# Two transposes move from TensorE to DMA: layer 1's mask and layer 3's result, with a retuned instruction order

## The chip, the cores and the metric

The kernel runs on one core of one Trainium2 chip. The metric is the device time of one execution in microseconds: the median of three runs, 3709.41 us before the change (3707.99 to 3712.8). A core has TensorE (PE in the profile; PEld is its weight load), VectorE (DVE), ScalarE (ACT), GpSimd (POOL), and SyncE (SP), which here issues all the transfers to 16 DMA engines.

## The reference, cut to what matters

The input is 64 graphs of 256 nodes with 256 features each, and a 256x256 adjacency for each graph. Four layers follow, each with a layer norm and ReLU ahead and a residual after. All of it is float32.

```python
for layer in (L0, L1, L2, L3):
    h = maximum(layernorm(x), 0)
    x = x + layer(h, adj)

# L0: attention with 8 heads, masked by adj, softmax over keys, output weights Wo
# L1: one head. e[i,j] = leaky_relu(f1[i] + f2[j]), masked by adj
#     softmax over axis 1 (over i, for each j), then h' = attention @ Wh, elu
# L2: three steps of message passing:  m = h W_l;  aggr = A^T m;  h = GRU(aggr, h)
# L3: four heads of 64 features:
f = (h @ W.T + b).reshape(B, N, H, c)
logits = leaky_relu(s_src[:, :, None, :] + s_dst[:, None, :, :])
probs  = softmax(where(adj == 1, logits, NEG_INF), axis=2)
out    = einsum('bijh,bjhc->bihc', probs, f).reshape(B, N, H * c)
```

Layer 1's softmax runs over i for each j. The kernel therefore holds j on the partitions, and needs the mask, which arrives with i on the partitions, turned. Layer 3's product comes out of TensorE with features on the partitions, and has to be turned before it is added to x, which has nodes on the partitions.

## The kernel before

The kernel takes two graphs at a time, a pair, 32 pairs in all. A tile `w4` is 128 partitions x 1024 float32: 4 tiles of 128 nodes (T = 4, two for each graph) by 256. Every piece of work is a task with the engine or engines that can do it, a modelled duration, and the buffers it reads and writes. When the kernel is built, a list scheduler with fixed constants puts the tasks in one static order for each engine, so that up to five pairs are in work at once and the long layer 2 fills gaps.

```python
# constants of the scheduler (times in us, and offsets in its priority)
SPARE, GRAIN = 5, 0.001          # w4 tiles kept back for the oldest pair
SLOW, MARGIN = 1.5, 0.4          # factor on a transfer's latency; extra ahead of SyncE
BACK = {"DVE": 0.3, "POOL": 0.6} # for work that two engines can do
PERIOD, REST = 698.4, 0
ON_PE = (-200, 1975, 7842, -3606)     # offset by layer, TensorE
ON_SP = (5643, 3540, 5173, -3294)
OTHERS = (2505, 934, 848, 4291)

SLOTS = {  # tag: (tiles, shape, type, reserve)
    "x": (5, [P, T * D], FP, 0),    "w4": (30, [P, T * D], FP, 9),
    "mask": (4, [P, T * N], BF, 1), "w2": (4, [P, N2], FP, 2),   # N2 = 512
    "ps": (8, [P, 512], FP, 2),     # PSUM banks
    ...
    "turn": (8, [P, T * N], FP, 0), # in DRAM
}
```

Most turns of attention matrices and of layer 2's state go through DRAM already: VectorE transposes 32x32 blocks, one transfer writes the tile out, and four transfers read it back with the blocks in their places. Only the last pair turns them on TensorE.

```python
def by_dma(l, p):
    return p < B // 2 - 1           # for all three steps of layer 2

def through_dram(e, eT):
    d = buf("turn")
    dma(d, e)                                              # 512 KB
    for b in range(4):                                     # 128 KB each
        dma(eT[32*b : 32*b+32].rearrange("p (a w) -> p a w", a=4),
            d[:, b*N : (b+1)*N].rearrange("(a j) w -> j a w", a=4))

def turn(e, eT):
    nc.vector.transpose(blocks(e), blocks(e)); through_dram(e, eT)
```

(The code above is shortened to its calls; `dma` stands for a task on SyncE.) Layer 1 builds a bfloat16 mask, computes the logits while a row of them goes through DRAM to all partitions, and turns the mask on TensorE into a PSUM bank:

```python
# layer 1
add((V, ..., m1 = (adj <= 0) * MASKED), reads=[at, hT], writes=[m1])     # bfloat16, [P, 4*256]
# ... Wh = h W; f1, f2; f1 as a row -> DRAM -> all partitions; e = prelu(f1 + f2)
psb = bank()
def turn_mask():
    for g in range(2):
        for cj in range(2):
            for ci in range(2):
                nc.tensor.transpose(                                     # L829
                    psm()[:, 2 * g + cj, ci * P : (ci + 1) * P],
                    tok(m1(), N)[:, 2 * g + ci, cj * P : (cj + 1) * P], identb)
add((PE, 8 * 0.058, turn_mask), reads=[m1, e], writes=[psb])
# logits: e = mask + e, with the row minimum of the negative, on VectorE, reading psm()
```

Layer 3 ends, for each graph g of the pair, with

```python
pso, oT = bank(), buf("w2")
add((PE, 1.86, product), reads=[*eT, (f, 2*g), (f, 2*g+1)], writes=[pso], claims=[oT])  # L1120
add(evict(N2, oT, pso), reads=[pso], writes=[oT])          # copy PSUM -> SBUF: ACT or VectorE
psq, o = bank(), buf("w2")
def back(psq=psq, oT=oT):
    for i in range(2):
        for k in range(2):
            nc.tensor.transpose(                                          # L1136
                psq()[:, i*D + k*P : i*D + (k+1)*P], oT()[:, k*N + i*P : k*N + (i+1)*P], ident)
add((PE, 4 * TURN, back), reads=[oT], writes=[psq], claims=[o, rz])
add((V, dve(N2), o = psq * rz), reads=[psq, rz], writes=[o])              # L1143, 1 / sum of exp
add(either(0.0, x_half += o), reads=[o], writes=[(xt, g)])                # L1148, VectorE or GpSimd
```

Of the kernel before, what the change touches and what calls it, by code (L numbers as in the profile page):

```python
# [9 lines left out]
FP = mybir.dt.float32  # L10
BF = mybir.dt.bfloat16
I32 = mybir.dt.int32
AF = mybir.ActivationFunctionType
ALU = mybir.AluOpType
AX = mybir.AxisListType

P = 128
# [21 lines left out]
class Plan:  # L39
# [11 lines left out]

    SPARE, GRAIN = 5, 0.001
    SLOW, MARGIN = 1.5, 0.4
    BACK = {"DVE": 0.3, "POOL": 0.6}


    PERIOD, REST = 698.4, 0
    ON_PE = (-200, 1975, 7842, -3606)  # L60
    ON_SP = (5643, 3540, 5173, -3294)
    OTHERS = (2505, 934, 848, 4291)

    def __init__(self, slots, spare):
        self.slots, self.spare = slots, spare
# [121 lines left out]
def tile_adj_preln_d4(  # L187
# [27 lines left out]
    nc = tc.nc  # L215
    B, N, D = x.shape
    NL = ggw.shape[0]
    H0, H3 = 8, a3.shape[0]
    D0, C3 = D // H0, D // H3
    assert N == 2 * P and D == 2 * P and B % 2 == 0 and H0 == 8 and H3 == 4  # L220
    T = 4
    N2 = 2 * N
# [3 lines left out]
    const = ctx.enter_context(tc.tile_pool(name="const", bufs=1))  # L226

    SLOTS = {
        "x": (5, [P, T * D], FP, 0),
        "w4": (30, [P, T * D], FP, 9),  # L230
        "f3": (2, [P, T, E3], FP, 0),
        "mask": (4, [P, T * N], BF, 1),
        "ps": (8, [P, 512], FP, 2),
        "w2": (4, [P, N2], FP, 2),
        "st": (4, [P, T, 6], FP, 1),
        "mv": (4, [P, T, 2], FP, 1),
        "rs": (4, [P, 2, T], FP, 1),
# [4 lines left out]
        "rows": (3, [T * H3, P], FP, 0),  # L242
        "dst": (4, [P, T, H3], FP, 0),
        "turn": (8, [P, T * N], FP, 0),
        "row1": (4, [N2], FP, 0),
        "row3": (4, [H3 * N2], FP, 0),
    }
# [4 lines left out]

    ident = const.tile([P, P], FP, name="ident")
    make_identity(nc, ident)
    identb = const.tile([P, P], BF, name="identb")
    nc.vector.tensor_copy(identb, ident)

    mhalf = const.tile([P, T], FP, name="mhalf")
    nc.vector.memset(mhalf, -0.5)

# [18 lines left out]
    dram = ctx.enter_context(tc.tile_pool(name="dram", bufs=1, space=bass.MemoryType.DRAM))  # L279
    for tag, (n, shape, dtype, _) in SLOTS.items():  # L280
        if tag not in tiles:
            tiles[tag] = [(dram if tag in ("row1", "row3", "turn") else work).tile(shape, dtype, name=f"{tag}_{i}") for i in range(n)]
    plan = Plan({tag: v[0] for tag, v in SLOTS.items()}, {tag: v[3] for tag, v in SLOTS.items()})

    def buf(tag):
        return Buf(tag, tiles[tag])
# [7 lines left out]
    def bank():  # L294
        return buf("ps")

    def dve(n):
        return 0.065 + n / 960.0
# [10 lines left out]
    def tok(ap, d=D):  # L309
        return ap.rearrange("p (t d) -> p t d", d=d)  # L310
# [4 lines left out]
    def evict(n, dst, src):  # L315

        return [
            (A, act(n), lambda: nc.scalar.copy(dst(), src())),  # L318
            (V, dve(n), lambda: nc.vector.tensor_copy(dst(), src())),
        ]  # L320
# [5 lines left out]
    add = plan.add  # L326
# [317 lines left out]
    def lowered(row, src, mask, scale, mn):  # L644

        nc.vector.tensor_tensor_reduce(row, src, mask, scale, 3.0e38, ALU.add, ALU.min, mn)  # L646
# [142 lines left out]
    def layer1(xt, p):  # L789
        at, hT = norm_relu_T(xt, p)  # L790
        m1 = buf("mask")
        add(
            (V, dve2(T * N), lambda: nc.vector.tensor_scalar(
                m1(), at().bitcast(I32), 0.0, MASKED, ALU.is_le, ALU.mult), True),
            reads=[at, hT], writes=[m1],
        )
        wh, f12 = w4(), buf("f12")
        for t in range(T):
            ps = bank()

            def product(t=t, ps=ps):
                for k in range(2):
                    mm(ps()[:, 0 : D + 2], chunk(hT, k, t), w1a[:, k, :], start=k == 0, stop=k == 1)  # L803

            add((PE, 0.88, product), reads=[hT, W1], writes=[ps], claims=[wh, f12])
            add(
                (V, 0.07, lambda t=t, ps=ps: nc.vector.tensor_copy(f12()[:, :, t], ps()[:, D : D + 2])),
                reads=[ps], writes=[(f12, t)],
            )
            add((A, act(D), lambda t=t, ps=ps: nc.scalar.copy(tok(wh())[:, t, :], ps()[:, 0:D])), reads=[ps], writes=[(wh, t)])  # L810
        f1 = buf("w2")
        to_all(buf("row1"), f12, lambda: f12()[:, 0], T, [f1])
        e = w4()
        for t in range(T):
            g = t // 2
            add(
                (A, act(N, 1), lambda t=t, g=g: nc.scalar.activation(
                    tok(e(), N)[:, t, :], f1()[:, g * N : (g + 1) * N], AF.Prelu,
                    bias=f12()[:, 1, t : t + 1], alpha=ALPHA)),
                reads=[f1, f12], writes=[(e, t)],  # L820
            )
        psb = bank()
        psm = lambda: psb().bitcast(BF).rearrange("p (t n) -> p t n", n=N)

        def turn_mask():
            for g in range(2):
                for cj in range(2):
                    for ci in range(2):
                        nc.tensor.transpose(  # L829
                            psm()[:, 2 * g + cj, ci * P : (ci + 1) * P], tok(m1(), N)[:, 2 * g + ci, cj * P : (cj + 1) * P], identb  # L830
                        )

        add((PE, 8 * 0.058, turn_mask), reads=[m1, e], writes=[psb])
        zs, mx, rz = buf("zs"), buf("mx"), buf("rz")
        for g in range(2):
            two = slice(2 * g, 2 * g + 2)
            parts = [(e, 2 * g), (e, 2 * g + 1)]
            def logits(g=g):
                for t in (2 * g, 2 * g + 1):
                    row = tok(e(), N)[:, t, :]  # L840
                    lowered(row, row, psm()[:, t, :], -1.0, mx()[:, t : t + 1])

            add((V, 2 * FUSED, logits), reads=[psb], writes=[*parts, (mx, g)])

            def exp(g=g):
                for t in (2 * g, 2 * g + 1):
                    row = tok(e(), N)[:, t, :]
                    nc.scalar.activation(row, row, AF.Exp, bias=mx()[:, t : t + 1], scale=-1.0, accum_out=zs()[:, t : t + 1])

            add((A, 2 * 0.494, exp), reads=[(mx, g)], writes=[*parts, (zs, g)])  # L850
            add((V, 0.18, lambda two=two: nc.vector.reciprocal(rz()[:, two], zs()[:, two])), reads=[(zs, g)], writes=[(rz, g)])
            def divided(g=g):
                for t in (2 * g, 2 * g + 1):
                    nc.scalar.mul(tok(wh())[:, t, :], tok(wh())[:, t, :], rz()[:, t : t + 1])

            add(
                [
                    (V, dve(N2), lambda two=two: nc.vector.tensor_tensor(
                        tok(wh())[:, two, :], tok(wh())[:, two, :], rz()[:, two].unsqueeze(2).to_broadcast([P, 2, D]), ALU.mult), True),
                    (A, 2 * act(N, 1), divided),  # L860
                ],
                reads=[(rz, g)], writes=[(wh, 2 * g), (wh, 2 * g + 1)],
            )
        for g in range(2):
            ps, ex = bank(), buf("w2")

            def product(g=g, ps=ps):
                for ci in range(2):
                    for cj in range(2):
                        mm(  # L870
                            ps()[:, ci * D : (ci + 1) * D],
                            tok(e(), N)[:, 2 * g + cj, ci * P : (ci + 1) * P],
                            tok(wh())[:, 2 * g + cj, :],
                            start=cj == 0,
                            stop=cj == 1,
                        )

            parts = [(b, 2 * g + c) for b in (e, wh) for c in range(2)]
            add((PE, 1.76, product), reads=parts, writes=[ps], claims=[ex])

            def exp_min(ps=ps, ex=ex):
                nc.scalar.activation(ex(), ps(), AF.Relu, scale=-1.0)
                nc.scalar.activation(ex(), ex(), AF.Exp, scale=-1.0)

            add((A, 2 * act(N2), exp_min), reads=[ps], writes=[ex])
            half = lambda g=g: xt()[:, g * N2 : (g + 1) * N2]
            add(
                (V, dve(N2), lambda ex=ex, half=half: nc.vector.tensor_add(half(), ex(), half()), True),
                reads=[ex], writes=[(xt, g)],
            )  # L890
            add(
                (V, dve(N2), lambda ps=ps, half=half: nc.vector.scalar_tensor_tensor(
                    half(), ps(), 0.0, half(), ALU.max, ALU.add)),
                reads=[ps], writes=[(xt, g)],
            )
# [151 lines left out]
    def layer3(xt, p):  # L1047
# [37 lines left out]
        for g in range(2):  # L1085
# [42 lines left out]

            add((PE, 1.86, product), reads=[*eT, (f, 2 * g), (f, 2 * g + 1)], writes=[pso], claims=[oT])
            add(evict(N2, oT, pso), reads=[pso], writes=[oT])  # L1130
            psq, o = bank(), buf("w2")

            def back(psq=psq, oT=oT):
# [13 lines left out]
            half = lambda g=g: xt()[:, g * N2 : (g + 1) * N2]  # L1147
            add(either(0.0, lambda eng, o=o, half=half: eng.tensor_add(half(), o(), half())), reads=[o], writes=[(xt, g)])  # L1148

    RANKS = (1.8, 3.9, 3.1)  # L1150
    for p in range(B // 2):
        plan.pair()
        plan.layer, xt = 0, buf("x")
# [53 lines left out]
```

## Time and profile before

Each group below is one line of the kernel and one form, from the trace's groups by line: how many, the mean duration of one, and the sum of the time in which that group kept its engine busy. Matmuls overlap, so the sum on TensorE can be less than count times mean.

| group | engine | count | mean ns | busy us |
|---|---|---|---|---|
| L829, transpose of the mask, bf16 128x128 | PE | 256 | 219 | 19.5 |
| L1136, transpose of layer 3's result, f32 128x128 | PE | 256 | 279 | 39.8 |
| L1143, times 1/sum, 128x512 | DVE | 64 | 680 | 43.5 |
| L1148, add to x, 128x512 | DVE | 34 | 709 | 24.1 |
| L1148, add to x, 128x512 | POOL | 30 | 1297 | 38.9 |
| L604, 32x32 transpose in place, 128x1024 | DVE | 380 | 1238 | 469.8 |
| L623, 32x32 transpose to other places, 128x1024 | DVE | 93 | 2068 | 192.3 |
| L958, gates of layer 2 | PE | 4608 | 595 | 2150.8 |

The 16 DMA engines moved 646.87 MB at a mean of 174 GB/s. The largest part is the turns: 473 writes of 512 KB (3.8 us from issue to landing, median) and 1892 reads of 128 KB (4.1 us). A load of x, 256 KB, lands in 3.6 us.

To read the page: the first block gives each engine's busy time and share, the slices cut the span into 40 equal parts and show busy tenths, and the timeline lists instructions in order of time. In brackets stands how long the engine was idle before and what ended that wait.

### The profile page before, as it was taken

To read this page: it belongs to the slowest core of one execution; us is meant where nothing else is said; L and a number is where in the kernel's file an instruction comes from. 1 tells how busy PE (TensorE), PEld (TensorE's weight loads), DVE (VectorE), ACT (ScalarE), POOL (GpSimd) and SP (SyncE) were. 2 spreads that over 40 slices of the span, in tenths; PEclk is the share of its full clock that TensorE was granted. 3 is DMA by queue.
4 is the path that set the end of the run, shared out by engine and by line. 5 is a ranking of instruction groups with operands and counts; after the bars stand their busy time and mean duration, and the time that the engine had idled before them with its cause. 6 is when DMAs were issued, how large, how long until landed. Compare 5 with 4: busy or idle time off the path is not lost.

```text
span 3707.6 us, 55796 instructions
## 1 busy us (share of the span) xinstructions
PE 3650.5 (98%) x16873; PEld 2077.9 (56%) x16873; DVE 2893.5 (78%) x7740; ACT 2585.7 (70%) x6993; POOL 485.8 (13%) x487
## 2 busy tenths in 40 slices
PE   8999999999999999999999999999999999999996
PEld 5655555555555555555555555555555555555553
DVE  7985787887777887778877778877788877788655
ACT  7974576777667776667776667776677766677545
POOL 2011111111111111111011111111111111110100
PEclk9999999999999999999999999999999999999998
DMA  8862566765567755567655577655677555676423
GB/s 237 230 165 70 154 182 190 214 176 167 164 166 204 215 165 161 159 189 208 194 163 161 165 198 215 171 168 161 172 205 209 169 158 159 192 208 187 126 80 103
DMA packets 465709, 646.87 MB, mean 174 GB/s; under 512 B 47360, under 2 KB 392576, under 8 KB 465408
## 3 DMA queue, kind: packets, MB, share of 16 engines
q1 hardware_dynamic: 465408, 643.29, 61.5%
q8 instruction: 135, 2.21, 0.3%
q14 instruction: 166, 1.36, 0.1%
HBM read 378.02 MB, written 265.09 MB: 173 GB/s over the span
## 4 chain that ended last, share of the span: by engine, by line
PE 81%; ACT 15%; DMA 1%; DVE 1%; issue 1%; SPq 0%; POOL 0%; ACTq 0%; DVEq 0%
PE ps L958 43%; PE ps L936 6%; PE ps L677 6%; PE ps L569 6%; ACT w L653 5%; ACT w L728 3%; PE ps L697 3%; PE ps L747 3%; PE ps L1068 3%; PE ps L540 3%; PE ps L803 3%; PE ps L1120 2%; PE ps L870 2%; ACT w L515 1%; ACT w L318 1%; ACT w L980 1%
## 5 line engine op out<-in xcount | busy, mean ns | idle before, releaser
L958 PE MATMUL ps<-w,whhT 128*128 128x512 f32 x2304 | 1076.0, 596 | 0.9 <-ACT w L318 0.9
L958 PE MATMUL ps<-w,giT 128*128 128x512 f32 x2304 | 1074.8, 594 | 0.0
L653 ACT ACTIVATE w<-w,mx 128x256 f32<-128x256 f32 x1536 | 758.3, 497 | 0.3 <-DVE mx L646 0.3
L958 PEld LDWEIGHTS ps<-w,giT 128*128 128x128 f32 x2304 | 428.6, 190 | 507.9 <-issue 493.5
L958 PEld LDWEIGHTS ps<-w,whhT 128*128 128x128 f32 x2304 | 420.6, 190 | 443.6 <-issue 407.6
L604 DVE STREAM_TRANSPOSE w<-w 128x1024 f32<-128x1024 f32 x380 | 469.8, 1238 | 53.5 <-ACT w L728 38.4
L318 ACT COPY w<-ps 128x512 f32<-128x512 f32 x520 | 293.1, 579 | 291.5 <-PE ps L677 111.8
L646 DVE CUSTOM_DVE_ANT_0 w<-ps,mask 128x256 f32<-128x256 f32 x1024 | 373.6, 418 | 29.2 <-PE ps L697 28.2
L1001 POOL TENSOR_TENSOR w<-w,w 128x512 f32<-128x512 f32 x97 | 148.7, 1533 | 1674.9 <-ACT w L996 1529.7
L728 ACT ACTIVATE w<-w,rz 128x256 f32<-128x256 f32 x718 | 308.4, 496 | 6.6 <-DVE rz L721 6.4
L653 ACT ACTIVATION_READ_ACCUMULATOR w<-w,mx 128x1 f32 x1536 | 291.4, 190 | 0.0
L985 DVE SCALAR_TENSOR_TENSOR w<-w,w 128x512 f32<-128x512 f32 x192 | 142.1, 740 | 185.2 <-ACT w L980 184.6
L1008 ACT ACTIVATE w<-ps,brz 128x512 f32<-128x512 f32 x192 | 129.4, 674 | 206.7 <-PE ps L958 135.5
L936 PEld LDWEIGHTS <-w 128*128 128x128 bf16 x2304 | 245.7, 128 | 45.6 <-issue 35.6
L936 PE MATMUL ps<-mask,w 128*128 128x256 bf16 x2304 | 268.2, 273 | 0.0
L980 ACT ACTIVATE w<-ps,brz 128x512 f32<-128x512 f32 x192 | 129.5, 675 | 157.7 <-PE ps L958 157.7
L1013 DVE SCALAR_TENSOR_TENSOR w<-w,w 128x512 f32<-128x512 f32 x192 | 129.8, 676 | 133.7 <-ACT w L1008 133.6
L515 ACT ACTIVATE w<-x,rs 128x256 f32<-128x256 f32 x390 | 206.8, 592 | 35.8 <-DVE rs L507 35.2
L1098 ACT ACTIVATE w<-w,f 128x256 f32<-128x256 f32 x512 | 224.7, 495 | 0.8 <-DMA w<-row 0.8
L996 ACT ACTIVATE w<-w,bih_sb 128x512 f32<-128x512 f32 x192 | 137.6, 717 | 106.0 <-DVE w L992 105.9
L488 DVE BATCH_NORM_STATS2 st<-x 128x6 f32<-128x256 f32 x512 | 188.9, 411 | 22.5 <-DMA x<-in_x_dram 19.4
L646 DVE CUSTOM_DVE_ANT_0 w<-w,mask 128x256 f32<-128x256 f32 x512 | 186.7, 421 | 11.2 <-ACT w L1098 11.2
(115 smaller groups left out, 5178.3 us busy)
## 6 DMA issues: line engine op xcount, KB each, us to landing
turn<-w SPq DMA_DIRECT2D x473, 512.0 KB, 3.8
w<-turn SPq DMA_DIRECT2D x1892, 128.0 KB, 4.1
w<-in_adj_dram SPq DMA_DIRECT2D x128, 512.0 KB, 7.1
w<-row SPq DMA_DIRECT2D x64, 512.0 KB, 5.0
x<-in_x_dram SPq DMA_DIRECT2D x64, 256.0 KB, 3.6
out_dram<-x SPq DMA_DIRECT2D x64, 256.0 KB, 2.2
w<-row SPq DMA_DIRECT2D x32, 256.0 KB, 3.2
w<-in_L_gnn_weight_dram SPq DMA_DIRECT2D x3, 256.0 KB, 8.1
```

Of the source, the lines that this page charges most:

```text
L318: (A, act(n), lambda: nc.scalar.copy(dst(), src())),
L488: nc.vector.bn_stats(st()[:, t, :], tok(xt())[:, t, :])
L515: nc.scalar.activation(tok(xn())[:, t, :], tok(xt())[:, t, :], func, bias=rs()[:, 1, t : t + 1], scale=rs()[:, 0, t : t + 1])
L569: mm(ps()[:, c * D : (c + 1) * D], chunk(src, k, 2 * g + c), rhs[:, k, :], start=k == 0, stop=k == 1)
L604: add((V, dve(T * N), lambda: nc.vector.transpose(blocks(), blocks())), writes=[e])
L646: nc.vector.tensor_tensor_reduce(row, src, mask, scale, 3.0e38, ALU.add, ALU.min, mn)
L653: nc.scalar.activation(row(e, r), row(e, r), AF.Exp, bias=mn()[:, r : r + 1], scale=-1.0, accum_out=zs()[:, z0(r) : z0(r) + 1])
L677: mm(ps(), w[:, k, o * P : (o + 1) * P], wide(hT, k), start=k == 0, stop=k == 1)
L728: op(row, row, rz()[:, r : r + 1])
L936: mm(ps()[:, g * N : (g + 1) * N], chunk_of(part(), h.mixed, t, o), tok(am(), N)[:, t, :], start=i == 0 and c == 0, stop=i == 2 and c == 1,)
L958: mm(ps(), w[:, k, c0 : c0 + P], wide(src, k), start=n == 0, stop=n == 2 * len(terms) - 1)
L1098: nc.scalar.activation(dst, src, AF.Prelu, bias=f()[:, t, D + h : D + h + 1], alpha=ALPHA)
```

## The change

The mask of layer 1 is turned by a single transposing DMA from SBUF to SBUF, and the logits read it there. Layer 3's result is turned in the way the other turns are: 32x32 blocks on VectorE, out to DRAM, back in four transfers. The multiplication by 1/sum and the addition to x become one operation, which takes 64 features of one head at a time because 1/sum differs by head and node tile. The last pair keeps the old path in layer 3. The purpose is to take both kinds of transposes off TensorE. Tiles are moved between pools to make room, and the scheduler's constants are set anew. The title that the change came with also names "layer 2's third step in T tiles"; the kernel before has it too, and no line of the diff touches it.

```diff
-    SPARE, GRAIN = 5, 0.001
-    SLOW, MARGIN = 1.5, 0.4
-    BACK = {"DVE": 0.3, "POOL": 0.6}
-    PERIOD, REST = 698.4, 0
-    ON_PE = (-200, 1975, 7842, -3606)
-    ON_SP = (5643, 3540, 5173, -3294)
-    OTHERS = (2505, 934, 848, 4291)
+    SPARE, GRAIN = 6, 0.001
+    SLOW, MARGIN = 1.4, 0
+    BACK = {"DVE": 0.3, "POOL": 1.1}
+    PERIOD, REST = 896, 0
+    ON_PE = (-1435, -211, 9269, -4344)
+    ON_SP = (6322, 2165, 5264, -1155)
+    OTHERS = (224, 368, 701, 3083)
...
-        "w4": (30, [P, T * D], FP, 9),
+        "w4": (28, [P, T * D], FP, 9),
-        "mask": (4, [P, T * N], BF, 1),
+        "mask": (6, [P, T * N], BF, 1),
-        "w2": (4, [P, N2], FP, 2),
+        "w2": (6, [P, N2], FP, 2),
+        "turn2": (4, [P, N2], FP, 0),          # in DRAM
...
-        psb = bank()
-        (turn_mask: eight nc.tensor.transpose, cut)
-        add((PE, 8 * 0.058, turn_mask), reads=[m1, e], writes=[psb])
+        m1T = buf("mask")
+        add(
+            (SP, 0.6, lambda: nc.sync.dma_start_transpose(m1T().rearrange("p (x q) -> p x q", x=2 * T), m1())),
+            reads=[m1], writes=[m1T], latency=5.0,
+        )
...
-                    lowered(row, row, psm()[:, t, :], -1.0, mx()[:, t : t + 1])
-            add((V, 2 * FUSED, logits), reads=[psb], writes=[*parts, (mx, g)])
+                    masked = m1T().rearrange("p (g i j q) -> p g j i q", g=2, i=2, j=2)[:, t // 2, t % 2]
+                    lowered(tok(row, P), tok(row, P), masked, -1.0, mx()[:, t : t + 1])
+            add((V, 2 * FUSED, logits, True), reads=[m1T], writes=[*parts, (mx, g)])
...
+            if not last:
+                e2, o, d = buf("w2"), buf("w2"), buf("turn2")
+                add(
+                    (V, dve(N2), lambda oT=oT, e2=e2: nc.vector.transpose(
+                        e2().rearrange("p (b x i) -> p b x i", b=4, i=32), oT().rearrange("p (x b j) -> p b x j", b=4, j=32))),
+                    reads=[oT], writes=[e2],
+                )
+                add((SP, 0.6, lambda d=d, e2=e2: nc.sync.dma_start(d(), e2())), reads=[e2], writes=[d], latency=3.2)
+                for b in range(4):
+                    add(
+                        (SP, 0.55, lambda b=b, d=d, o=o: nc.sync.dma_start(
+                            o()[32 * b : 32 * b + 32, :].rearrange("p (a w) -> p a w", a=4),
+                            d()[:, b * P : (b + 1) * P].rearrange("(a j) w -> j a w", a=4))),
+                        reads=[d], writes=[(o, b)], latency=3.0, claims=[rz],
+                    )
+                for c in range(2):
+                    def to_x(c=c, g=g, o=o, rz=rz):
+                        for h in range(H3):
+                            ap = o().rearrange("p (j a x i) -> p j x a i", j=2, a=2, i=32)[:, h % 2, 2 * (h // 2) + c]
+                            xh = tok(xt())[:, 2 * g + c, h * C3 : (h + 1) * C3].rearrange("p (a i) -> p a i", a=2)
+                            nc.vector.scalar_tensor_tensor(
+                                xh, ap, rz()[:, H3 * c + h : H3 * c + h + 1], xh, ALU.mult, ALU.add
+                            )
+                    add((V, H3 * 0.14, to_x, True), reads=[o, rz], writes=[(xt, g)])
+                continue
...
-    RANKS = (1.8, 3.9, 3.1)          # when the weights of layers 1 to 3 are prepared
+    RANKS = (3, 3.6, 1.3)
```

More of the change, by code (lines that the diff above doesn't have):

```diff
@@ L254, in tile_adj_preln_d4 @@
     make_identity(nc, ident)
-    identb = const.tile([P, P], BF, name="identb")
-    nc.vector.tensor_copy(identb, ident)
     mhalf = const.tile([P, T], FP, name="mhalf")
@@ L281, in tile_adj_preln_d4 @@
         if tag not in tiles:
-            tiles[tag] = [(dram if tag in ("row1", "row3", "turn") else work).tile(shape, dtype, name=f"{tag}_{i}") for i in range(n)]
+            tiles[tag] = [(dram if tag in ("row1", "row3", "turn", "turn2") else work).tile(shape, dtype, name=f"{tag}_{i}") for i in range(n)]
     plan = Plan({tag: v[0] for tag, v in SLOTS.items()}, {tag: v[3] for tag, v in SLOTS.items()})
@@ L821, in layer1 @@
             )
-        psb = bank()
[L823 to L831, printed above, removed]
-        add((PE, 8 * 0.058, turn_mask), reads=[m1, e], writes=[psb])
+        m1T = buf("mask")
[3 more added lines that the diff above has]
+        )
         zs, mx, rz = buf("zs"), buf("mx"), buf("rz")
```

## The prediction

> **What bounds the kernel now.** I read the page's busy shares first, then the slices, then cut the middle of the run into pieces one pair long, and last read TensorE in order of time around the instructions that the change removes.
>
> ```profile
> span 3707.6 us, 55796 instructions
> PE 3650.5 (98%) x16873; PEld 2077.9 (56%) x16873; DVE 2893.5 (78%) x7740; ACT 2585.7 (70%) x6993; POOL 485.8 (13%) x487
> ...
> PE   8999999999999999999999999999999999999996
> ```
>
> TensorE is busy 3650.5 of 3707.6 us. Of its 57.1 us of idle time the slices put most at the two ends: only the first slice (8) and the last (6) fall below nine tenths. The engine's order repeats: the mask transposes of layer 1 (L829) start at 1014.07, 1126.71 and 1239.38 us, so one pair of graphs takes 112.67 us. I asked for the busy time by stretch in three such pieces (columns: stretch and length, busy PE, weight load, DVE, ACT, POOL, clock, DMA share, GB/s):
>
> ```profile
> 1014.00:1126.70 112.70, 112.48 (x523) 63.82 (x522) 89.76 (x241) 80.30 (x220) 15.15 (x15) 1.00 0.64 180
> 1126.70:1239.30 112.60, 112.36 (x523) 63.81 (x522) 89.67 (x241) 80.20 (x220) 15.13 (x15) 1.00 0.63 180
> 1239.30:1352.00 112.70, 112.41 (x523) 63.82 (x522) 90.00 (x241) 80.22 (x219) 15.13 (x15) 1.00 0.65 180
> ```
>
> In the steady state TensorE idles about 0.25 us per pair at full clock, DVE has 22.8 us to spare, ACT 32, and the DMA engines are 64% busy. So a pair costs what TensorE's instruction stream costs, and every microsecond taken out of that stream should come off the time, 32 times over, until something else has to wait.
>
> The removed instructions have to be priced by pitch and not by duration, because consecutive matmuls overlap. The timeline gives the pitch (start, length, instruction):
>
> ```profile
> 1014.07 0.61 PE L829 MATMUL ps<-identb,mask 128*128 128x128 bf16 x8
> 1014.51 1.94 PE L958 MATMUL ps<-w,giT 128*128 128x512 f32 x4
> ...
> 1025.12 1.99 PE L870 MATMUL ps<-w,w 128*128 128x256 f32 x8
> 1026.96 0.60 PE L1136 MATMUL ps<-ident,w 128*128 128x128 f32 x4
> 1027.39 2.78 PE L936 MATMUL ps<-mask,w 128*128 128x256 bf16 x24
> ...
> 1042.30 1.98 PE L958 MATMUL ps<-w,giT 128*128 128x512 f32 x4
> 1044.50 0.66 PE L1136 MATMUL ps<-ident,w 128*128 128x128 f32 x4 [0.22 <-ACT w L318]
> 1045.00 1.88 PE L958 MATMUL ps<-w,giT 128*128 128x512 f32 x4
> ```
>
> Eight mask transposes take 1014.51 - 1014.07 = 0.44 us. A group of four fp32 transposes (L1136) takes 0.43 or 0.50 us to the next start. The second group also arrives late: the four matmuls before it take 2.20 us from start to start, where four of the same line take 1.72 elsewhere. So its hand-over, a wait for ACT's copy plus an emptied pipeline, costs 0.48 us more. The first group's hand-over costs about 0.10 (1.84 against 1.73 for the eight L870 matmuls elsewhere).
>
> [...] the timeline shows a pitch of 0.11 us in fp32 and 0.055 us in bf16, and I count the pitch. [...] No transposing DMA is in this trace; a plain load of the same 256 KB (x) lands in 3.6 us. [...] 98% means here that the instruction stream has no gaps, not that it could not be shorter.
>
> **The change part by part.**
>
> Part 1, layer 1's mask, all 32 pairs. Removed: eight bf16 transposes, 0.445 us of pitch per pair, 14.2 us in all. Added: one transposing DMA of 256 KB per pair. The masked logits then read SBUF instead of PSUM, for the same price (415 ns with the PSUM mask, 421 ns for the layer-3 form that reads only SBUF). The DMA starts when the mask is built. The logits must meanwhile wait for the row that goes out to DRAM (2 KB, about 1.4 us by its neighbour's median) and comes back to all partitions (3.2 us), after a TensorE transpose and an ACT copy. [...] Off the path.
>
> Part 2, layer 3's result, 31 pairs of two groups (the last pair keeps the old way). Removed per pair on TensorE: 0.43 + 0.50 = 0.93 us of pitch and 0.58 us of hand-over. That is 28.8 us certain and 18.0 us that return only if the schedule finds no other place to stumble. I count half of it, 9 us.
>
> On DVE, 62 groups. Removed: the multiply by 1/z, 680 ns each (42 us), and DVE's share of the additions, 34 of 64 at 709 ns (about 23 us). Added: a 32x32 transpose of 512 elements with a scattered destination; the same form at 1024 takes 2068 ns (L623), so about 1.03 us, 64 us in all. And eight scalar_tensor_tensor of 64 elements. The traced forms give 168 ns at 4 elements and 676 at 512, 1.0 ns per element, so about 228 ns each: 496 x 0.228 = 113 us. Net +112 us: DVE goes from 2893 to about 3005 us, from 89.8 to 93.4 us per pair, with a pair then lasting about 111. GpSimd loses its 30 additions (38.9 us), and two PSUM banks per pair come free earlier.
>
> DMA, both parts: 62 x (256 KB out and 256 KB back) + 32 x 256 KB = 41 MB on 643, 6.4%. At the same cost per byte the mean share rises from 61.5% to about 66% of a slightly shorter span. SyncE issues 62 x 5 + 32 = 342 more transfers beside about 2,800. An issue takes 0.3 to 0.45 us of its sequencer, so 100 to 155 us more, some 5 us per pair. Its own waits (905.8 us for the rows alone) show room.
>
> Part 3, the schedule. The instruction order is drawn up when the kernel is built, by a list scheduler with fixed constants. All of them are retuned, and buffers move: w4 from 30 to 28 with 6 kept in reserve instead of 5, mask and w2 from 4 to 6. I can't price that from the trace; I take it as a retuning to the new work that keeps TensorE fed. [...]
>
> Sum on TensorE: 14.2 + 28.8 + 9 = 52 us. I give 4 us back for the ends and for new stumbles: 3709.4 - 52 + 4 = **3661 us**, 1.3% less.
>
> **The rivals.**
>
> Rival A, SyncE or the DMA engines hold things up. [...] For it: five more transfers per group, the first part of the run with a DMA share of 0.83, and a transposing DMA whose price no run here shows; if it held the queue for 20 us, the turns behind it would come late and TensorE would run dry. Against it: 64% DMA share in the steady state, and TensorE hardly waits for any turn today (DMA w<-turn ends 5.3 us of L1120's weight-load waits and 2.3 of L747's in the whole run). Result: 3690 to 3800.
>
> Rival B, DVE becomes the bound. Its stretches reach 86 of 100 us, and 100 to 200 us shows 91. If the extra 3.6 us per pair landed there in full where TensorE waits for DVE, 31 x 3.6 = 112 us would cancel the gain: 3710 to 3770. Against it: 93.4 of 111 us leaves DVE 17 us per pair, and layer 3's result is needed by nobody on TensorE until the next load into its x buffer.
>
> Rival C, fewer free tiles. With w4 at 28 and 6 reserved, turns may start later and layer 2, the filler of every gap, may run out. Each gap of 0.5 us per pair costs 16 us: 3670 to 3700.
>
> Rival D, the hand-overs vanish altogether and the retuned order smooths the ends. The first 50 us and the last 107 hold 13.9 and 31.0 us of idle TensorE. All of 61 us and some of the ends: 3635 to 3650.
>
> **Range and chances.** A, B and C push upward and D downward; most of the mass is between full pitch savings with all of the hand-overs (3648) and pitch savings with some new stalls (3680). I take 3640 to 3700. Two per cent faster is 3635, which needs D in full: 0.05. Two per cent slower is 3784, which needs A or B at their worst: 0.03. The rest, 0.92, within 2%.
>
> **What would show it.** Right: L829 and L1136 nearly gone (8 calls of L1136's line left for the last pair, none for the mask), TensorE still at 98%, a repeat distance near 111 us, DVE near 3005 us with a group of 496 short scalar_tensor_tensor near 0.23 us, DMA share near 66%[...]. Wrong: TensorE below 97% with waits on a turn or on the transposed mask (A), on DVE (B), or a consistent gap that ends with a tile's release (C); or short DVE instructions far from 0.23 us. The whole prediction fails if the new order leaves TensorE idle for more than 45 us in the middle of the run.

## The result, and the profile after

The changed kernel takes **3663.48 us** (median of four runs, 3663.3 to 3667.32) against 3710.72 us before on the same chip: a ratio of 0.9876, with a 95% interval of 0.9858 to 0.9893. The prediction was 3661 us in a range of 3640 to 3700.

The head of the page after:

```profile
span 3661.3 us, 55666 instructions
PE 3600.6 (98%) x16369; PEld 2042.1 (56%) x16369; DVE 2951.6 (81%) x8204; ACT 2587.2 (71%) x6995; POOL 428.1 (12%) x455
...
PE   8999999999999999999999999999999999999996
```

TensorE's busy time fell by 49.9 us (3650.5 to 3600.6) and its idle time rose by 3.6 (57.1 to 60.7). These two make up the 46.3 us between the two profiled spans. TensorE's share stays at 98%, so the share alone shows nothing of what happened.

Busy time by stretch, in two pieces one pair long (stretch and length, busy PE, weight load, DVE, ACT, POOL, clock, DMA share, GB/s):

```profile
1007.70:1118.70 111.00, 111.00 (x507) 62.88 (x506) 91.89 (x256) 80.62 (x221) 13.10 (x14) 1.00 0.70 195
1118.70:1229.80 111.10, 111.10 (x507) 62.87 (x506) 92.22 (x256) 80.72 (x221) 13.05 (x14) 1.00 0.70 195
```

A pair now takes 111.05 us where it took 112.67, and TensorE has no idle time left in it; before it had some 0.25 us. That is 1.62 us for each pair, or 50 us if it is counted for 31 pairs, of which 4 us did not come. Only 24 repeats in the middle are equal (from 648 to 3352 us before, from 643 to 3308 us after). They became shorter by 38.4 us; the other eight pairs, at the two ends, gave the remaining 7.9 us of the 46.3. The last 111 us, for example, hold 37.4 us of idle TensorE, where the last 107 us before held 31.0.

One line of the page before was not read for the prediction: the chain of work that ended last, by engine. Here it is for the kernel before, and then for the changed one.

```profile
PE 81%; ACT 15%; DMA 1%; DVE 1%; issue 1%; SPq 0%; POOL 0%; ACTq 0%; DVEq 0%
```

```profile
PE 95%; DVE 2%; ACT 2%; DMA 1%; issue 0%; SPq 0%; POOL 0%; POOLq 0%; DVEq 0%; ACTq 0%
```

In the kernel before, 15% of the chain ran over ScalarE, although TensorE was busy 98% of the time. The experiments show what that means.

### The profile page after: what moved, and what is told of

It reads as the page before. It is cut to its first block, busy times and chain, and to the rows that moved or that the text cites. A ratio compares the mean times of both kernels' runs of the same rounds, so it can differ in the third digit from the quotient of the medians.

```text
span 3661.3 us, 55666 instructions
## 1 busy us (share of the span) xinstructions
PE 3600.6 (98%) x16369; PEld 2042.1 (56%) x16369; DVE 2951.6 (81%) x8204; ACT 2587.2 (71%) x6995; POOL 428.1 (12%) x455
## 3 DMA queue, kind: packets, MB, share of 16 engines
q1 hardware_dynamic: 543840, 684.21, 66.3%
## 4 chain that ended last, share of the span: by engine, by line
PE 95%; DVE 2%; ACT 2%; DMA 1%; issue 0%; SPq 0%; POOL 0%; POOLq 0%; DVEq 0%; ACTq 0%
PE ps L951 53%; PE ps L929 7%; PE ps L567 6%; PE ps L675 6%; PE ps L695 4%; PE ps L1113 3%; PE ps L863 3%; PE ps L1061 3%; PE ps L745 3%; PE ps L801 3%; PE ps L538 3%; ACT w L651 1%; PE ps L411 0%; DVE w L602 0%; DVE w L644 0%
## 5 line engine op out<-in xcount | busy, mean ns | idle before, releaser
L602 DVE STREAM_TRANSPOSE w<-w 128x1024 f32<-128x1024 f32 x380 | 467.7, 1236 | 40.2 <-ACT w L726 29.9
L316 ACT COPY w<-ps 128x512 f32<-128x512 f32 x547 | 302.7, 579 | 132.7 <-PE ps L929 52.6
L994 POOL TENSOR_TENSOR w<-w,w 128x512 f32<-128x512 f32 x95 | 131.0, 1379 | 1821.4 <-ACT w L989 1403.0
L726 ACT ACTIVATE w<-w,rz 128x256 f32<-128x256 f32 x688 | 299.5, 500 | 15.3 <-DVE rz L719 15.3
L978 DVE SCALAR_TENSOR_TENSOR w<-w,w 128x512 f32<-128x512 f32 x192 | 132.8, 692 | 181.4 <-ACT w L973 181.2
L550 ACT ACTIVATE w<-ps 128x512 f32<-128x512 f32 x187 | 104.3, 595 | 168.8 <-PE ps L538 168.8
```

The lines of the kernel that those rows point to most:

```text
L602: add((V, dve(T * N), lambda: nc.vector.transpose(blocks(), blocks())), writes=[e])
L726: op(row, row, rz()[:, r : r + 1])
```

## The experiments

Twelve kernels were run, each beside the kernel before. "Pair" is the distance in the timeline between the same instruction of one pair and the next, in the steady state.

| kernel | us | ratio to before (95%) | pair, us |
|---|---|---|---|
| before | 3709 to 3711 | | 112.67 |
| changed | 3663.5 | 0.9876 (0.9858 to 0.9893) | 111.05 |
| b_nomask | 3708.2 | 0.9999 (0.999 to 1.0007) | 112.68 |
| b_noback | 3671.4 | 0.9899 (0.9884 to 0.9914) | 111.33 |
| b_neither | 3656.7 | 0.9861 (0.9846 to 0.9876) | 110.83 |
| b_nomask_dvecopy | 3700.8 | 0.9979 (0.9971 to 0.9987) | 112.24 |
| a_nodma | 3664.3 | 0.9882 (0.9865 to 0.9898) | 111.05 |
| a_nopool | 3666.2 | 0.9883 (0.9868 to 0.9898) | 111.05 |
| a_oldconst | 3785.4 | 1.0205 (1.0188 to 1.0222) | irregular |
| b_newconst | 3760.0 | 1.0137 (1.0122 to 1.0152) | irregular |
| mask_only | 3679.7 | 0.9918 (0.9901 to 0.9934) | 111.56 |
| result_only | 3681.4 | 0.9921 (0.9906 to 0.9936) | 111.28 |
| m1_tuned | 3669.0 | 0.9888 (0.9873 to 0.9903) | 110.43 |
| m1_late | 3652.4 | 0.9846 (0.983 to 0.9863) | 110.44 |

### What the removed instructions are worth in the old order

The first three leave TensorE's transposes out of the kernel before and keep every other instruction in its place. The list scheduler still plans the empty tasks, so only the instructions are gone.

```diff
 # b_nomask
         def turn_mask():
+            return
-                    lowered(row, row, psm()[:, t, :], -1.0, mx()[:, t : t + 1])
+                    lowered(row, row, plain, -1.0, mx()[:, t : t + 1])      # a tile of zeros
 # b_noback
             def back(psq=psq, oT=oT):
+                return
-                (V, dve(N2), lambda psq=psq, ...: o = psq * rz
+                (V, dve(N2), lambda psq=oT, ...: o = oT * rz
 # b_neither: both
```

> The kernel before, with the same order of every other instruction. Left out: the eight bfloat16 transposes of layer 1's mask for each pair; the logits add a tile of zeros instead, so layer 1 is not masked. Theory (TensorE's instruction stream is the time, and the mask costs its pitch): 32 x 0.445 = 14.2 us less, 3696 us. Rival (the transposes sit in gaps that TensorE has anyway, or the time is set by DVE or transfers): under 5 us.

> The kernel before, same order. Left out: the four fp32 transposes at the end of layer 3 (all 64 groups); the multiplication reads the unturned product, so the result is in the wrong places. Theory: 0.93 us of pitch for each pair, 30 us in 32 pairs, plus the hand-over of 0.58 us (18.6 us) if it goes with them: 30 to 48 us, 3662 to 3680 us. Rival A (the hand-over is a wait that the next instruction inherits): 30 us only. Rival B (DVE or transfers bind): under 10 us.

> The kernel before, same order, both kinds of transposes left out. Theory: the two savings add up, 44 to 62 us, 3648 to 3665 us, which is what a change that only removes work could have brought with this order. If DVE or the transfers were close behind TensorE, the sum would be less than the two parts.

Measured: without the mask's transposes **nothing** (3708.2 us, a ratio of 0.9999), without the result's 37.6 us, without both 52.2 us. So the mask's transposes were worth 14.7 us only when the others were gone too (3671.4 to 3656.7). That is close to their pitch, 32 x 0.445 = 14.2. The expectation for b_nomask, 14.2 us less, was a miss.

The timeline of b_nomask at the second group of layer 3's transposes (L1139 there, L1136 in the kernel before) shows where the time went (start, length, instruction, and in brackets the idle time before and what ended it):

```profile
1042.00 1.98 PE L961 MATMUL ps<-w,giT 128*128 128x512 f32 x4
1044.72 0.66 PE L1139 MATMUL ps<-ident,w 128*128 128x128 f32 x4 [0.74 <-ACT w L320]
1045.21 1.88 PE L961 MATMUL ps<-w,giT 128*128 128x512 f32 x4
```

The idle time before this group was 0.22 us in the kernel before and is 0.74 here. TensorE arrives earlier and waits longer for ScalarE's copy of layer 3's product; over the run that wait grew from 6.7 to 19.5 us. The period was not set by TensorE's stream alone but by a loop that passes through ScalarE once for each pair. In the kernel before, the chain of work leaves TensorE and runs over ScalarE from 1030.19 to 1044.50 us (start, length, what):

```profile
1027.56 2.63 PE ps L936 x24
1030.19 0.56 ACT w L318
1030.75 1.20 ACT w L653 x5
...
1043.98 0.48 ACT w L318
1044.50 0.66 PE ps L1136 x4
```

In that stretch ScalarE is busy 14.27 of 14.30 us, although over the whole pair it is busy 80.3 of 112.7. A mean over the pair hid it, and TensorE's gap of 0.22 us was too short to stand out.

This chain alone does not explain b_nomask: it still counts the mask's transposes (L829, 1014.23 us) on its TensorE part, before it turns to ScalarE. But ScalarE's unbroken stretch begins much earlier. One repeat later, in the kernel before, it starts with a copy that waited for layer 1's product (L803) and ends with the copy of layer 3's product:

```profile
1100.24 0.37 ACT L810 COPY w<-ps 128x256 f32<-128x256 f32 x1 [1.41 <-PE ps L803]
...
1156.54 0.57 ACT L318 COPY w<-ps 128x512 f32<-128x512 f32 x1
```

From 1100.24 us, where the first starts, to 1157.01 us, where the instruction after the second starts, no ScalarE instruction waits: the engine is busy 56.71 of 56.77 us. TensorE works beside it and is just as full (56.69 us busy), so the two ways take almost the same time. The mask's transposes, at 1126.71 us, lie on TensorE's way. Without them the chain of b_nomask takes ScalarE's way (L805 is layer 1's product there, L320 the copy's line):

```profile
1043.21 0.98 ACT w L517 x2
1045.38 5.15 PE ps L961 x12
...
1099.35 1.08 PE ps L805 x4
1100.83 1.97 ACT w L655 x8
...
1125.56 1.47 ACT w L655 x6
```

Its share of ScalarE grows from 15% to 36%. So the loop is about 56 us of TensorE and 57 us of ScalarE; the mask's transposes are not on it, and the second group of result transposes is.

Once the transposes that wait for the copy are gone (b_noback), the loop is open: the chain is 95% TensorE, and removed TensorE work comes off in full (the mask's 14.7 us).

To test the loop, b_nomask was run again with that one copy moved from ScalarE to VectorE.

```diff
 # b_nomask_dvecopy, on top of b_nomask
-            add(evict(N2, oT, pso), ...)        # planned on ScalarE or VectorE
+            add(the same plan, but nc.vector.tensor_copy(oT(), pso()) in both cases, ...)
```

> The kernel before without layer 1's mask transposes (as in the run that gave nothing), and the copy of layer 3's product out of PSUM, on which the result's transposes wait, done by VectorE wherever ScalarE did it; order otherwise the same. Theory (the period of 112.68 us was a loop through ScalarE's queue and that copy, so that removed TensorE work only lengthened the wait): the loop is cut and the mask's 14 us appear, with some of the 0.5 us of hand-over for each pair: 3680 to 3696 us. Rival (the mask's transposes were free for some other reason): 3705 us or more.

Measured: 3700.8 us, less than b_nomask's 3708.2 but short of the 3680 to 3696 that were expected. A pair takes 112.24 us, 0.44 less than in b_nomask, and TensorE's wait at this place fell from 0.74 to 0.24 us. VectorE's copy now ends it:

```profile
1042.19 0.66 PE L1139 MATMUL ps<-ident,w 128*128 128x128 f32 x4 [0.24 <-DVE w L1133]
```

So the loop did pass through this copy. It was shortened and not cut: 35% of the chain still runs over ScalarE. That 0.44 us equals the mask's pitch does not show that just this pitch came back, since the copy that left ScalarE had kept it for 0.47 us, from its start at 1156.54 us to the next one at 1157.01 (kernel before). The 14 us of the expectation counted 32 pairs. The 24 equal repeats gained 10.3 us (2704.4 to 2694.1), of which about 1 was lost again at the two ends: the profiled runs differ by 9.1 us, the medians by 7.4.

### Whether what was added costs anything

```diff
 # a_nodma: the changed kernel, same order
-    (V, dve(N2), nc.vector.transpose(e2, oT))           +    (V, dve(N2), nothing)
-    (SP, 0.6, nc.sync.dma_start(d(), e2()))             +    (SP, 0.6, nothing)
-    (SP, 0.55, nc.sync.dma_start(o()[32*b:..], d()..))  +    (SP, 0.55, nothing)
-    (SP, 0.6, nc.sync.dma_start_transpose(m1T, m1))     +    (SP, 0.6, nothing)
```

> The changed kernel, same order. Left out: all that the change adds except the short multiplications: layer 3's 32x32 transposes (44 us of DVE), its 62 writes and 248 reads, and the 32 transposing transfers of the mask. The operations read old contents of the same tiles. Theory (all of this lies beside TensorE's stream): within 5 us of the changed kernel, 3659 to 3664 us. Rival (SyncE's issues, 1.7 us for each transposing one, and the transfers delay turns that TensorE waits for): 15 us less or more.

Measured: 3664.3 us against 3663.5, and the same 111.05 us for a pair. The 32x32 transposes, all 342 added transfers and their issues on SyncE cost no time that can be measured here. Rival A of the prediction is excluded for this order. Near its end the changed kernel does wait twice for turns (L1113, 8.31 and 6.64 us), but those are turns of attention matrices that the kernel before has too, and a_nodma waits 14.3 us at the same place. The short multiplications stayed in this run, so for them only the trace speaks: the changed kernel's chain holds 2% of VectorE in all.

What VectorE's additions cost VectorE itself can be read in the groups by form of the changed kernel (count | busy us, mean ns | idle before):

```profile
L1146 DVE SCALAR_TENSOR_TENSOR x<-w,rz,x 128x64 f32<-128x64 f32 x496 | 103.7, 276 | 4.0 <-DMA w<-turn 4.0
L1128 DVE STREAM_TRANSPOSE w<-w 128x512 f32<-128x512 f32 x62 | 43.6, 703 | 11.4 <-ACT w L316 11.3
L634 DVE TENSOR_SCALAR mask<-w 128x512 bf16<-128x512 int32 x126 | 107.0, 891 | 1.2 <-DMA w<-in_adj_dram 1.2
```

The third line is none of the change's doing: the masks of layers 0 and 3 took 49.9 us in the kernel before (438 ns each), at an unchanged line of the program. The timeline of the changed kernel shows GpSimd's additions over them:

```profile
1061.40 1.52 POOL L1036 TENSOR_TENSOR x<-x,w 128x512 f32<-128x512 f32 x1
1061.50 3.11 DVE L634 TENSOR_SCALAR mask<-w 128x512 bf16<-128x512 int32 x2
1062.88 1.45 POOL L994 TENSOR_TENSOR w<-w,w 128x512 f32<-128x512 f32 x1
```

Two mask instructions last 3.11 us under two GpSimd additions; 10 us later, with GpSimd idle, two take 0.76. So the additions were moved.

```diff
 # a_nopool: the changed kernel, same order
-        return [(G, pool(N2) + more, lambda: do(nc.gpsimd), True), ...]
+        return [(G, pool(N2) + more, lambda: do(nc.vector), True), ...]
```

> The changed kernel with the additions that the plan gives to GpSimd (layer 2's and layer 3's) done by VectorE, in the same order. Theory (VectorE's mask instruction takes 1.49 us in place of 0.42 where it coincides with a GpSimd addition, a stall that costs the time nothing as it lies beside TensorE): the mask instruction's mean falls to about 0.42 us, VectorE's busy time rises by less than the 127 moved additions at 0.68 to 1.07 us, and the time stays within 5 us of 3663. Rival (that stall is what is left between the changed kernel and the floor): 10 us less or more.

The mask instructions then take 418 ns at the median and 428 at most. VectorE's busy time rises by only 16.5 us (2951.6 to 2968.1) although it does 127 more additions, and the time is 3666.2 us with the same pair of 111.05. So the stall is real, it comes with GpSimd's additions and goes with them, and it costs nothing here: the pair does not change.

### What the new order is worth

```diff
 # a_oldconst: the changed kernel        # b_newconst: the kernel before
-    PERIOD, REST = 896, 0              -    PERIOD, REST = 698.4, 0
+    PERIOD, REST = 698.4, 0            +    PERIOD, REST = 896, 0
     and all other constants and RANKS likewise; buffers as they were
```

> The changed kernel with the scheduler's constants of the kernel before (buffers as in the changed kernel). Theory (the constants are fitted to one set of tasks; the removed work pays only with an order fitted to it): slower than the kernel before, about 3775 us, since the scheduler's own planned end is 3760 us where it was 3693 for the kernel before, which then took 3709. Rival (the saving is work that is gone, whatever the order): about 3664 to 3680 us.

> The kernel before with the scheduler's constants of the changed kernel (its own buffers). Theory (constants fitted to one set of tasks): about 3770 us, the planned end being 3754. Rival (the new constants are better in themselves and are the source of the gain): under 3700 us.

Measured: 3785.4 us and 3760.0 us. The change with the old constants is 2% **slower** than the kernel before, and the new constants on the old kernel 1.4% slower. Each set of constants belongs to one set of tasks. In a_oldconst TensorE's busy time is 3646.3 us, almost as before, although the same instructions were removed as in the changed kernel; its mean granted clock over the run is 0.985 against 0.993, and its idle time is 138.9 us against 60.7. The loss belongs to the order that the old constants plan for the new tasks: with the old order itself kept, leaving both kinds of transposes out gained 52.2 us (b_neither).

So the parts were also run alone, with constants fitted to each set by the scheduler's own planned end.

```diff
 # mask_only: kernel before + transposing transfer of the mask; w4 29, mask 6; fitted constants
 # result_only: changed kernel with turn_mask on TensorE again; fitted constants
```

> The kernel before with the first part of the change alone (layer 1's mask by a transposing transfer; mask tiles 6, w4 tiles 29) and constants of the scheduler fitted to that set of tasks (planned end 3680 us; 3693 for the kernel before, which takes 3709). Theory (the mask's pitch of 14 us is won once the order is fitted anew, although leaving it out in the old order gave nothing): 3690 to 3698 us. Rival (the mask's transposes are worth nothing while layer 3's transposes stay on TensorE): 3705 us or more.

> The changed kernel with the mask turned on TensorE again, that is the second part alone (layer 3's result through DRAM), with constants fitted to that set (planned end 3672 us). Theory: pitch and part of the hand-over, 30 to 38 us less than before: 3671 to 3680 us, and about 14 us more than the changed kernel. Rival (the return through DRAM needs the mask's PSUM bank and the rest of the change): 3700 us or more.

Measured: 3679.7 and 3681.4 us, that is 29.8 and 28.1 us less than before, where the two together (the changed kernel) give 47. result_only lies 1.4 us above the range expected for it, and 18 us above the changed kernel where 14 were expected. The mask's part brings twice its pitch and is faster than the 3690 to 3698 us expected. In mask_only the two groups of result transposes are still on TensorE (L1130 there), but they no longer wait:

```profile
1042.85 1.88 PE L952 MATMUL ps<-w,giT 128*128 128x512 f32 x4
1044.57 0.60 PE L1130 MATMUL ps<-ident,w 128*128 128x128 f32 x4
1045.10 1.93 PE L747 MATMUL ps<-w,w 128*32 128x256 f32 x32
```

From the four matmuls to the transposes it is 1.72 us, the bare pitch; it was 2.20 in the kernel before. The hand-over of 0.48 us was a matter of the order and did not come with the transposes as such. Of the 1.11 us that a pair gains in mask_only, 0.445 is pitch, and the hand-overs account for most of the other 0.66. One rival stays untested: no run gives the kernel before, its tasks unchanged, constants that were fitted anew with the same effort. How much of the 47 us an order alone could have brought is therefore not known.

### One step further

Layer 1's normalised input takes eight more fp32 transposes on TensorE for each pair. The same turn through VectorE and DRAM was put in their place, in 31 pairs, and then from the eighth pair on only; constants fitted to each.

```diff
 # m1_tuned; in m1_late with 7 <= p as well
+        mixed = plan.layer in (1,) and p < B // 2 - 1
+        if mixed:
+            turn_chunks(xn, hT)                 # 32x32 blocks, DRAM; ReLU goes into the scaling
-        for i in range(2):
+        for i in range(2) if not mixed else ():
     def chunk(hT, k, t):
+        if hT.mixed:
+            return hT().rearrange("p (m x) -> p x m", x=2 * T)[:, 2 * t + k]
```

> One step further in the same direction: the changed kernel with layer 1's normalised input also turned by VectorE's 32x32 blocks and DRAM in place of eight fp32 transposes on TensorE and two copies out of PSUM (31 pairs), with constants fitted to that set (planned end 3638 us; 3655 for the changed kernel, which takes 3663). Theory (TensorE's stream is the time, and VectorE at 81% and the transfers at 66% still have room): 31 x 0.87 = 27 us of pitch, of which the plan keeps 16: 3640 to 3650 us. Rival (VectorE, with 64 us more, or the transfers, with 5% more bytes, now bind): 3660 us or more.

> The step further again (layer 1's normalised input turned through DRAM), but only from the eighth pair on, with constants fitted to that (planned end 3633 us; 3638 for the same step from the first pair, which took 3669). In that run a pair took 110.43 us in the steady state, 0.62 less than in the changed kernel, and the gain was lost in the first 600 us. Theory (the steady state pays 0.62 us for each pair, and the start is left as it was): 24 x 0.62 = 15 us less than the changed kernel, 3645 to 3655 us. Rival (with VectorE at 84% in the steady state the order that is planned no longer holds): 3663 us or more.

m1_tuned took 3669.0 us, a miss: slower than the changed kernel. Its pair is shorter, 110.43 us, but by 0.62 us and not by 0.87. The missing part is in the weight loads of the product that follows, which now read every eighth element. Here are those loads in m1_tuned, and then in the changed kernel:

```profile
L806 PEld LDWEIGHTS ps<-w1a,w 128*128 128x128 f32 x512 | 126.5, 330 | 11.5 <-issue 6.9 <-DMA w<-turn 0.2 <-DVE st L486 0.2
```

```profile
L801 PEld LDWEIGHTS ps<-w1a,w 128*128 128x128 f32 x512 | 95.0, 190 | 33.4 <-issue 15.2 <-DVE mx L644 6.0 <-ACT w L1091 0.2
```

A load takes 330 ns in place of 190. The sixteen products of a pair take 3.91 us from start to start where they took 3.68 (0.96 and 2.72 in two groups there; 3.68 in one group in the kernel before), so 0.23 of the 0.87 us goes back. The rest was lost at the start: in the first 600 us TensorE is busy 569.8 us against 577.5 in the changed kernel, and its clock over 100 to 600 us falls to 0.93, 0.98, 1.00, 1.00 and 0.97, where the changed kernel has 1.00 throughout.

m1_late leaves the start as it was and takes **3652.4 us**: 11 us less than the changed kernel and the fastest here. Its pair takes 110.44 us.

## Why the prediction was right

The total and the repeat distance held, and so did the core of the mechanism: work leaves TensorE, and what is added runs beside it. The sum is close: 52 us on TensorE less 4 for the ends predicted, against 50 (the steady gain counted for 31 pairs) less 4 measured. Part of this closeness is luck. The 9 us for hand-overs and the 4 for the ends were guesses, and two terms were right for a reason other than the one given.

**"Every microsecond taken out of that stream should come off the time"** is the step that failed. For the old order it is false: b_nomask took 0.445 us for each pair out of the stream and gained nothing, because 57 us of unbroken ScalarE work ran beside that part of the stream and the repeat was as long by that way. The step had rested on the small idle time in the pair, and the chain of waits, with 15% on ScalarE, had not been read. It is true once the waiting transposes are gone, which the change also does, and so the sum survived.

**Part 1, 14.2 us**: 0 alone in the old order, 14.7 once the result's transposes are gone, 29.8 alone in an order fitted anew. The pitch itself, 0.445 us for each pair, was read correctly.

**Part 2, 28.8 us of pitch and half of 18.0 of hand-over**: 37.6 us in the old order, where all 32 pairs leave the transposes out: 29.8 of pitch and 7.8 more. That fits 28.8 + 9, but the half was a guess. The nature of the hand-over was misread: the larger one was where ScalarE's loop held TensorE back, and mask_only's order is free of it with the transposes still there. Of the 0.48 us that it cost in the kernel before, 0.22 is the wait for ScalarE's copy; the other 0.26 is overlap that was lost, since the four matmuls before it last 1.98 us and elsewhere start the next instruction after 1.72. In the changed kernel a pair gained 1.62 us: 1.38 of pitch, and 0.24 of the 0.58.

**VectorE**, predicted at 3005 us, came to 2951.6. The transposes of 512 elements take 703 ns and not half of 2068: the row that the prediction scaled down writes to every eighth element, and the new one writes runs of 32. The short multiplications last 276 ns each where 228 were estimated, but consecutive ones overlap, so that each keeps VectorE busy for only 209 ns. Other lines moved as much in both directions: the masks gained 57 us as shown, and the second subtraction in layer 2 (L923 before, L916 after) lost 43 (161.8 to 118.4).

**Transfers**: 40.9 MB more (41 predicted) and a share of 66.3% (66 predicted). The transposing transfer holds SyncE's sequencer for 1.74 us at the median, where 0.3 to 0.45 were assumed for every issue. It makes no difference here (a_nodma: 3664.3 us without it against 3663.5). How long it takes to land is not recorded in this trace and stays open; that it lies off the path was the author's estimate, which the equal time of a_nodma supports.

**Part 3, the schedule**, for which the prediction gave no price, is the condition of everything else: without it the change loses 76 us instead of gaining 47. No rival of the prediction named an unfitted order, and none named ScalarE.

Rival A did not come true (a_nodma). Rival B did not either: VectorE has 92 us of work in a pair of 111, and TensorE has no idle time. Of C nothing is seen in the pair. Of D, the changed kernel kept 0.24 of the 0.58 us of hand-over, and its ends got no smoother.

## What to carry to other kernels

A busy share of 98% says that an engine is nearly always at work, not that it sets the pace: in the kernel before, 15% of the chain of waits ran over ScalarE. Read that chain as well. Where it leaves the busy engine at a point in every repeat, look how far back the other engine has worked without a break (57 us here). Work taken from the busy engine beside that stretch only lengthened its wait in b_nomask: 0.445 us of pitch went, the wait grew from 0.22 to 0.74 us, and the time stayed. Leave an instruction out in an unchanged order to learn its worth there, and expect another worth in another order. Where a static order is fitted to a set of tasks, compare two sets only after both have been fitted; here the same change is 2% slower or 1.2% faster.

## What the runs showed of the hardware that was not expected

- A VectorE mask instruction (128x512, int32 to bfloat16) takes 418 ns alone (median of a_nopool) and about 1.5 us while GpSimd adds two float32 tiles (3.11 us for two in the changed kernel); with those additions moved to VectorE no instance exceeds 428 ns.
- A transposing transfer of 256 KB from SBUF to SBUF occupies SyncE's sequencer for 1.24 to 2.58 us (median 1.74; changed kernel, L823), a plain one in the kernel before for 0.34 (writes of turns, median) to 0.43 (their reads, median).
- A float32 weight load that reads every eighth element takes 330 ns (m1_tuned, L806) in place of 190 (changed kernel, L801), and 16 products of 258 columns behind such loads take 3.91 us in place of 3.68.
- VectorE's 32x32 transpose takes 2070 ns for 1024 elements where the destination takes every eighth element (L621), and 703 ns for 512 where it takes runs of 32 elements (L1128); in place, 1024 take 1236 ns (L602). At 1024 elements the scattered destination adds 834 ns to the transpose in place.
